# Two attention layers on one core: other credit thresholds for side steps in cross attention, and a longer hold on the keys' staging

## The chip, the cores and the metric

The kernel runs on 1 core of one Trainium2 chip. The metric is the device time of one execution in microseconds (us). A round below is one step of the kernel's main loop, not a measurement. Three timed runs of the kernel before gave 2921.99 (median), 2918.47 and 2926.42 us.

## The reference

Two layers, each with self attention, cross attention and a gated feed-forward part, on x of 4 x 512 x 320 with a context of 4 x 1601 x 192. There are 20 heads of 16 columns.

```python
h1 = _ln(x, n1_g, n1_b)
x = _attn(h1, h1, q1, k1, v1, o1_w, o1_b, heads) + x
h2 = _ln(x, n2_g, n2_b)
x = _attn(h2, context, q2, k2, v2, o2_w, o2_b, heads) + x
h3 = _ln(x, n3_g, n3_b)
a, g = jnp.split(h3 @ ff_w1 + ff_b1, 2, axis=-1)
x = a * gelu(g) @ ff_w2 + ff_b2 + x
```

`_attn` projects queries, keys and values, takes the softmax of the scaled products per head, and projects the result. In cross attention keys and values come from the context, so there are 1601 of them for each of the 4 batch entries.

## The kernel before, in words

**Units.** The work is a list of units (lines 364 to 371). An attention unit, called a visit here, is one batch entry b and one group g of four heads; there are 5 groups, so 20 visits make a layer's self attention and 20 its cross attention. Each head of a group has 32 rows of its own in the arrays, so that four heads run side by side.

**Rounds.** `main` (line 1311) goes through a visit's keys in chunks of 128: 4 rounds in self attention, 13 in cross attention. One round holds

- the scores of the chunk for four heads (`st`, line 1324: two products of keys and queries, in a high and a low part, and one that subtracts the row's maximum), each followed by an exponential on ScalarE into a `pr` tile (line 1334);
- beside them products for the maxima of the next visits (`sps`, lines 1076 and 1101), each reduced on VectorE (lines 1087 and 1111). `giver` (line 1623) hands these out;
- the product of the exponentials of the chunk before with the values (`av`, line 1350), which ScalarE copies out as `vo` (line 1369) and GpSimd adds to `o` (line 1370);
- then the side steps, by `steps(None, ...)` (line 1399).

`clock["round"]` counts half rounds: in cross attention two for each pass of the loop.

**Side steps.** What a visit needs of projections is queued in chains, first in, first out (line 396). The heavy ones run on TensorE and are evacuated by ScalarE or VectorE:

- `keys_of_context` (line 964): a visit's keys in four parts (`kps`, line 972). ScalarE copies each part into the staging `room["halves"]`; after the fourth, GpSimd splits it into a high and a low part (lines 827 and 828), and two DMAs (line 876) carry the halves to the visit's `kT`, once that is free;
- `queries` (line 938, `qps`, line 947), in the same chain behind the visit's keys;
- `values` (line 1025, `vps`, line 1035) of a batch entry, 13 chunks in two parts of 8 and 12 heads. The visits g = 0 and g = 2 read freshly made values, and line 1346 runs whatever is still missing ahead of the `av` that reads it;
- `project` (line 1243, `ops`, line 1250), the output projection, 8 steps for each batch entry.

Each entry has a cost in us of the planner, written into the code, a due date in half rounds, and a test that says whether it can go. Light entries (norms, transposes, DMAs) cost 0.01 or nothing.

**Credit.** `tick` (line 483) adds `pace()` to the credit at each half round, kept between -2 and 4. `pace()` (line 465) is the largest, over all due dates, of the summed cost of the entries due until then divided by the half rounds left. `steps` (line 487) takes the entry that is due first, and runs it if the credit reaches a threshold; running one takes its cost off the credit. In attention rounds the threshold is 0.5 of the entry's cost for the first heavy step of a round, 0.75 for the second, 1.5 for the third, and a credit of 3.0 for any more:

```python
share = (2.2, 1.1) if beside else (9.0, 9.0) if beside is False else (0.5, 0.75, 1.5)
least = cost * share[done] if done < len(share) else 3.0
if clock["credit"] < (3.0 if beside is False else least):
    break
```

**The keys' staging.** There is one. `pending["k"]` counts the moves of keys that are waiting to be issued; the first part of the next visit's keys can go when there are none (`keys_free`, line 890), that is from the moment at which both DMAs have been issued. `carry` (line 808) issues the moves, at the end of `steps`.

Of the kernel before, what the change touches and what calls it, by code (L numbers as in the profile page):

```python
# [78 lines left out]
def kernel(ctx: ExitStack, tc: tile.TileContext, x, context, ws, out):  # L79
# [59 lines left out]
    room = {"turn": 0, "first": 0}  # L139
# [68 lines left out]
    def now(fs):  # L208
        for f in fs:
            f()  # L210
# [183 lines left out]


    chains = {n: deque() for n in ("divide", "project", "norm", "scale", "context", "early", "proj", "values")}
    clock = {"round": 0, "credit": 0.0, "lights": 0, "tiles": None, "ff": False}
    ALIKE = ("project", "early", "proj", "values")
    LIGHT = 0.01
    stage = [0] * B  # L400
# [50 lines left out]
    def pick():  # L451
        heads = [
            (q[0][1] + late_by(n), n)
            for n, q in chains.items()
            if q and q[0][2]() and q[0][3]() and (q[0][0][0] != LIGHT or clock["lights"])
        ]
        return min(heads)[1] if heads else None

    def run(chain):
        costs, _, ready, _, f = chains[chain].popleft()  # L460
        assert ready(), chain
        f()
        clock["credit"] -= sum(costs)
# [19 lines left out]
    def tick():  # L483
        clock["round"] += 1
        clock["credit"] = max(-2.0, min(4.0, clock["credit"] + pace()))

    def steps(beside, lights=1):


        tick()  # L490
        clock["lights"] = lights
        clock["tiles"] = True if beside is None else None
        done = 0
        while True:
            name = pick()
            if name is None:
                break
            cost = sum(chains[name][0][0])
            if cost >= 0.1:
                share = (2.2, 1.1) if beside else (9.0, 9.0) if beside is False else (0.5, 0.75, 1.5)  # L500
                least = cost * share[done] if done < len(share) else 3.0
                if clock["credit"] < (3.0 if beside is False else least):
                    break
                done += 1
                if clock["tiles"] is not None:
                    clock["tiles"] = name in ALIKE
            run(name)
            if cost == LIGHT:
                clock["lights"] -= 1
        clock["tiles"] = None  # L510
        carry()
# [200 lines left out]
    def until_normed(test):  # L712
        while not test():
            if chains["scale"] and chains["scale"][0][2]():
                run("scale")
            elif bands:
                bands.popleft()[1]()
            else:
                run("norm")
# [72 lines left out]
    def lead(u):  # L792

        if u.i == 0:
            return 0
        return units[u.i - (AHEAD - 1 if u.early else 2 if u.m == 0 else 1)].start
# [8 lines left out]
    pending = {"q": 0, "k": 0}  # L805
    movers = []

    def carry():

        room = 4  # L810
        for _, what, u in sorted(movers):
            todo = u.moves[what]
            while todo and todo[0][1]() and clock["round"] >= u.moving[what] + todo[0][2] and room > 0:
                room -= 2
                todo.popleft()[0]()
            if not todo:
                movers.remove((u.i, what, u))
        while errands and room > 0 and clock["round"] >= errands[0][0] and errands[0][1]():
            errands.popleft()[2]()
        few = 6 if clock["ff"] else min(room + 1, 3)  # L820
        while bands and few > 0 and clock["round"] >= bands[0][0]:
            bands.popleft()[1]()
            few -= 1
# [6 lines left out]
    def add_proj(u):  # L830
# [35 lines left out]
        def move(of, pairs, may, gap=0):  # L866

            def f():
                pending[of] -= 1
                u.moving[of] = clock["round"]  # L870
                for to, src in pairs():
                    queue = nc.sync
                    if start["on"]:
                        queue = (nc.sync, nc.scalar)[room["first"] % 2]
                        room["first"] += 1
                    queue.dma_start(out=to.bitcast(F32), in_=src)
                u.open -= 1
                if not u.open:
                    u.when = -9 if start["on"] else clock["round"]

            pending[of] += 1
            u.moves[of].append((f, may, gap))
            u.moving[of] = clock["round"]
            if (u.i, of, u) not in movers:
                movers.append((u.i, of, u))
# [2 lines left out]
            return len(users) < 2 or not users[-2].moves["q"] and (start["on"] or clock["round"] >= users[-2].moving["q"] + 4)  # L888

        def keys_free():  # L890
            return not pending["k"]

        def move_queries(halves, cols, may, gap):
            n = halves.shape[0]
# [384 lines left out]
    def flush():  # L1279
        for f in late:  # L1280
            f()
        late.clear()
# [28 lines left out]
    def main(u, give, nxt):  # L1311
# [62 lines left out]
        for c in range(u.nch):  # L1374
# [21 lines left out]
            if last and c == u.nch - 1:  # L1396
                for _ in range(4):
                    begin(units[u.i + 1])
            steps(None, 1 if extra or c == u.nch - 1 else 2)
            for i, e in enumerate(extra[1:]):  # L1400
                if i and next_cost() is not None:
# [14 lines left out]
    def add_norms(i):  # L1416

        while norms and norms[0].i <= i + ((1 if norms[0].b else 3) if norms[0].kind == "ff" else AHEAD + 1 if norms[0].early else 8):
            u = norms.popleft()
            if u.kind == "ff":  # L1420
                add_norm(u.l, u.b, 2, lambda t, u=u: setattr(u, "hT", t), lambda u=u: u in ff_read, u.start - (4 if u.b else 40))
            else:

                def done(u=u):
                    return u.made["q"] == G and (u.cross or u.made["k"] == G and u.vmade[1] == u.nch)

                due = lead(u) - ((10 if u.early else 12) if u.cross else 28)
                add_norm(u.l, u.b, int(u.cross), lambda t, u=u: u.own.update(h=t), done, due)
# [30 lines left out]
    def ff_main(u, give, nxt):  # L1459
        done = 0  # L1460

        def beside(room, n):

            nonlocal done
            if room:
                for extra in give(done, True)[1]:
                    round_of(extra)
            done += n
            if done == u.steps - 1 and nxt is not None and nxt.kind != "ff":
                max_reduce(nxt)  # L1470
                max_end(nxt)
            steps(True)
            for _ in range(n - 1):
                steps(False)
# [86 lines left out]
    def before(u):  # L1561

        if u.kind == "cross" and u.g == 1 and u.b + 1 < B or u.kind == "self" and u.m == EARLY - 3:
            b = u.b + 1 if u.cross else 0
            if u.l == 0:
                load_context(b, 0)
                load_context(b, 1)
                if u.cross:
                    add_turned(b, u.start + 46, 6)
        if u.kind == "self" and u.m == 0 and u.l:  # L1570
            take_rooms(u.l)
        if u.kind == "cross" and u.m == B * G - 1:
            take_weights()
            loads.extend(load_first(u.l, (0, 1, 3)) + load_ff(u.l)[2])
        if u.kind == "cross" and u.m == B * G - 3:
            take_rests()
            small, rests, _ = load_ff(u.l)
            loads.extend(small + rests)
        if u.kind == "cross" and u.m == B * G - 2:
            loads.extend(load_first(u.l, (4, 2)))  # L1580
        if u.kind == "self" and u.m == EARLY - 1 and u.l == 0:
            add_turned(0, units[u.i + 1].start + 22, 2)
        if u.kind == "self" and u.m == EARLY:

            add_context(0, lambda s: units[u.i - u.m + B * G].own.update(kv=s["cT"]), u.start + 36, yes)
# [142 lines left out]
    for i, u in enumerate(units):  # L1728
        nxt = units[i + 1] if i + 1 < len(units) else None
        before(u)  # L1730
        if u.kind == "ff":

            flush()
            now(loads)
            loads.clear()
            until_normed(lambda: u.hT is not None)
        clock["ff"] = u.kind == "ff"
        add_norms(i)
        for k in (3, SOON, AHEAD):
            v = units[i + k] if i + k < len(units) else None  # L1740
            if v is not None and v.kind != "ff" and k == (SOON if not v.cross else AHEAD if v.early else 3):
                add_proj(v)
                if v.g == 0:
                    add_values(v)
        (ff_main if u.kind == "ff" else main)(u, giver(u), nxt)
# [27 lines left out]
```

## Time and profile before

| | |
|---|---|
| median of 3 timed runs | 2921.99 us (2918.47 to 2926.42) |
| the profiled execution | 2916.39 us, span 2914.6 us |
| mean granted TensorE clock | 0.995 |
| instructions | 83287 |

The span runs from the first instruction to the last. PE is TensorE, PEld its weight loader, which runs beside it; DVE is VectorE, ACT ScalarE, POOL GpSimd, SP the queue that issues the DMAs. A matmul that waits in the pipeline is counted as busy. The lines of a group name the line of the kernel, the engine, the operation, what is written from what is read, and the number of them; then the busy time, the mean of one in ns, and the idle time of the engine before them with what ended it. A line of the timeline gives the start, the time it took, the engine and the instruction, and in brackets the idle time before it with what ended it. A line of the waits gives who waited for whom, the sum in us, the number, and the longest.

By the timeline the self attention of layer 0 takes about the first 370 us of the span. The windows used below, 375 to 1137 us and in layer 1 1915 to 2575 us, hold the cross attention rounds in which side steps still go; behind them the last visits of each layer run without any.

### The profile page before, as it was taken

To read this page: it belongs to the slowest core of one execution; us is meant where nothing else is said; L and a number is where in the kernel's file an instruction comes from. 1 tells how busy PE (TensorE), PEld (TensorE's weight loads), DVE (VectorE), ACT (ScalarE), POOL (GpSimd) and SP (SyncE) were. 2 spreads that over 40 slices of the span, in tenths; PEclk is the share of its full clock that TensorE was granted. 3 is DMA by queue.
4 is the path that set the end of the run, shared out by engine and by line. 5 is a ranking of instruction groups with operands and counts; after the bars stand their busy time and mean duration, and the time that the engine had idled before them with its cause. 6 is when DMAs were issued, how large, how long until landed. Compare 5 with 4: busy or idle time off the path is not lost.

```text
span 2914.6 us, 83287 instructions
## 1 busy us (share of the span) xinstructions
PE 2860.1 (98%) x35018; PEld 1545.0 (53%) x35018; DVE 1975.7 (68%) x3752; ACT 1950.2 (67%) x4033; POOL 1299.4 (45%) x1409
## 2 busy tenths in 40 slices
PE   8999999999999999999999999999999999999999
PEld 4445555555555555355554555555555555544554
DVE  7777888788788878323257678787778878862221
ACT  3777678888888888500138776788888888893000
POOL 3656345555645545211125653455455464551100
PEclk8999999999999999999999999999999999999999
DMA  4444223232132222200113432222221122122000
GB/s 106 114 121 102 72 71 97 58 89 60 48 96 59 55 54 63 85 17 11 36 45 88 109 99 67 61 64 57 54 66 47 50 73 60 45 65 67 23 21 13
DMA packets 163495, 188.59 MB, mean 65 GB/s; under 512 B 61989, under 2 KB 109105, under 8 KB 163121
## 3 DMA queue, kind: packets, MB, share of 16 engines
q1 hardware_dynamic: 162616, 181.69, 24.4%
q8 instruction: 275, 4.51, 0.6%
q10 hardware_dynamic: 472, 1.58, 0.2%
q14 instruction: 100, 0.81, 0.1%
q0 software_dynamic: 32, 0.00, 0.0%
HBM read 55.76 MB, written 29.36 MB: 29 GB/s over the span
## 4 chain that ended last, share of the span: by engine, by line
PE 88%; DVE 4%; POOL 4%; DMA 2%; issue 1%; ACT 1%; SPq 0%; POOLq 0%; ACTq 0%; DVEq 0%
PE av L1350 22%; PE st L1324 20%; PE fps L1435 10%; PE sps L1076 9%; PE yps L1542 6%; PE vps L1035 5%; PE kps L972 4%; PE ops L1250 3%; PE qkps L908 3%; PE fps L1495 3%; DVE nmax L1087 2%; PE qps L947 2%; PE sps L1101 1%; POOL o L1370 1%; DVE pm L1087 1%
## 5 line engine op out<-in xcount | busy, mean ns | idle before, releaser
L1334 ACT ACTIVATE pr<-st 128x512 f32<-128x512 f32 (+1 forms) x2720 | 1405.0, 603 | 321.4 <-PE st L1324 292.0
L1087 DVE TENSOR_REDUCE pm<-sps 128x1 f32<-128x512 f32 (+1 forms) x1920 | 1148.3, 660 | 244.6 <-PE sps L1076 239.0
L1370 POOL TENSOR_TENSOR o<-o,vo 128x512 f32<-128x512 f32 x576 | 739.9, 1285 | 930.3 <-ACT vo L1369 909.7
L1076 PE MATMUL sps<-kT,q 32*128 32x450 f32 (+1 forms) x4800 | 870.6, 422 | 8.1 <-DMA q<-halves 4.4
L1324 PE MATMUL st<-q,kT 32*128 32x512 f32 (+1 forms) x5120 | 788.9, 419 | 0.8 <-ACT o L1364 0.4
L1350 PE MATMUL av<-pr,vals 128*32 128x512 f32 (+1 forms) x5440 | 734.2, 606 | 27.3 <-ACT pr L1334 5.4
L1324 PEld LDWEIGHTS st<-q,kT 32*128 32x128 f32 (+1 forms) x5120 | 447.0, 180 | 293.0 <-issue 112.7
L1324 PE MATMUL st<-nrows,ones 32*128 32x512 f32 (+1 forms) x2720 | 560.6, 398 | 4.5 <-DMA nrows<-turned 4.4
L1087 DVE TENSOR_REDUCE nmax<-sps 128x1 f32<-128x512 f32 x640 | 397.2, 682 | 118.0 <-PE sps L1076 114.2
L1076 PEld LDWEIGHTS sps<-kT,q 32*128 32x128 f32 x4800 | 434.0, 184 | 67.1 <-ACT pr L1334 11.7
L1369 ACT COPY vo<-av 128x512 f32<-128x512 f32 x576 | 351.7, 611 | 14.7 <-PE av L1350 8.7
L1506 ACT ACTIVATE gl<-fps,b 128x512 f32<-128x512 f32 x80 | 54.8, 687 | 408.8 <-PE fps L1495 299.1
L1435 PE MATMUL fps<-hT,w 128*128 128x512 f32 x640 | 283.1, 597 | 0.0
L1350 PEld LDWEIGHTS av<-pr,vals 128*32 128x32 f32 (+1 forms) x5440 | 111.0, 108 | 300.3 <-DVE pm L1087 185.2
L1324 PEld LDWEIGHTS st<-nrows,ones 32*128 32x128 f32 (+1 forms) x2720 | 262.3, 180 | 14.5 <-DMA nrows<-turned 6.1
L1507 DVE SCALAR_TENSOR_TENSOR hid<-fps,b,gl 128x512 f32<-128x512 f32 x80 | 59.7, 748 | 248.1 <-ACT gl L1506 246.0
L1435 PEld LDWEIGHTS fps<-hT,w 128*128 128x128 f32 x640 | 119.2, 190 | 155.1 <-issue 152.2
L1542 PE MATMUL yps<-w,hid 128*128 128x320 f32 x640 | 175.7, 434 | 0.0
L1542 PEld LDWEIGHTS yps<-w,hid 128*128 128x128 f32 x640 | 120.5, 190 | 56.3 <-ACT gl L1506 5.3
L1250 PEld LDWEIGHTS ops<-wo,aT 112*32 112x32 f32 (+1 forms) x3072 | 98.2, 110 | 59.2 <-issue 28.5
L1250 PE MATMUL ops<-wo,aT 112*32 112x160 f32 (+1 forms) x3072 | 123.8, 299 | 3.7 <-POOL aT L1232 2.7
L1111 DVE TENSOR_REDUCE pm<-sps 128x4 f32<-128x508 f32 x160 | 98.9, 680 | 37.5 <-PE sps L1101 34.8
(89 smaller groups left out, 2453.7 us busy)
## 6 DMA issues: line engine op xcount, KB each, us to landing
kT<-stages SPq DMA_DIRECT2D x80, 400.5 KB
oway<-o SPq DMA_DIRECT2D x80, 256.0 KB
q<-halves SPq DMA_DIRECT2D x80, 256.0 KB
q<-halves SPq DMA_DIRECT2D x27, 512.0 KB
kT<-halves SPq DMA_DIRECT2D x40, 256.0 KB
aT<-oway SPq DMA_DIRECT2D x32, 224.0 KB
rT<-rway SPq DMA_DIRECT2D x32, 224.0 KB
hT<-hturned SPq DMA_DIRECT2D x96, 64.0 KB
```

Of the source, the lines that this page charges most:

```text
L972: nc.tensor.matmul(ps[(i * GT + f) * SLOT : (i * GT + f + 1) * SLOT, :w], lhsT=wk2[:, k, u.g * GD + f * SLOT : u.g * GD + (f + 1) * SLOT], ...
L1035: nc.tensor.matmul(ps[f : f + m, :w], lhsT=u.kvT[:n, k, at + f : at + f + m], rhs=wv[:n, k, h0 * DH : h1 * DH], start=(k == 0), stop=(k == ...
L1076: nc.tensor.matmul(own[0][:, :w], lhsT=u.queries(slice(j * SLOT, (j + 1) * SLOT), e, t), rhs=u.kT[j * SLOT : (j + 1) * SLOT, u.k0 + at : u ...
L1087: nc.vector.tensor_reduce(to, own[0][:, :w], AX.X, ALU.max)
L1250: nc.tensor.matmul(ps[f : f + m, : D // 2], lhsT=aT[:n, k, f * NQ + t * SLOT : f * NQ + t * SLOT + m], rhs=wo[:n, k, cols], start=(k == 0) ...
L1324: nc.tensor.matmul(own[0][:r, :], lhsT=ones[rows, :r] if e == 2 else u.keys(rows, c), rhs=u.rows[rows, :] if e == 2 else u.queries(rows, e ...
L1334: nc.scalar.activation(p[:r], own[0][:r], AF.Exp)
L1350: nc.tensor.matmul(ps[j * SLOT : (j + 1) * SLOT, :], lhsT=columns_of[:r, head : head + SLOT], rhs=pr.pop((c, j))[:r, :], start=True, stop= ...
L1369: nc.scalar.copy(vo, ps)
L1370: nc.gpsimd.tensor_tensor(u.o, u.o, vo, ALU.add)
L1435: nc.tensor.matmul(ps, lhsT=w1[:, k, i * FF + c * P : i * FF + (c + 1) * P], rhs=natural(u.hT[:, k]), start=start, stop=stop,)
L1542: nc.tensor.matmul(ps[:, :D], lhsT=hid[c][:, t * P : (t + 1) * P], rhs=w2[:, c, :], start=(c == 0), stop=(c == NHC - 1),)
```

## The change

In cross attention (`clock["cross"]`, set for each unit) the first heavy step of a round goes when the credit is at least -0.5, whatever its cost; a second when the credit left is at least 1.5 times its cost; a third and any further one at a credit of 3.0. The other stages keep their thresholds. And the first part of a visit's keys also waits until four half rounds have gone by since the last move of keys was issued (`room["sent"]`).

```diff
-    clock = {"round": 0, "credit": 0.0, "lights": 0, "tiles": None, "ff": False}
+    clock = {"round": 0, "credit": 0.0, "lights": 0, "tiles": None, "ff": False, "cross": False}
...
                 least = cost * share[done] if done < len(share) else 3.0
+                if beside is None and clock["cross"]:
+                    least = (-0.5, 1.5 * cost, 3.0)[min(done, 2)]
                 if clock["credit"] < (3.0 if beside is False else least):
                     break
...
             def f():
                 pending[of] -= 1
+                if of == "k":
+                    room["sent"] = clock["round"]
                 u.moving[of] = clock["round"]
...
         def keys_free():
-            return not pending["k"]
+            return not pending["k"] and clock["round"] >= room.get("sent", -9) + 4
...
         clock["ff"] = u.kind == "ff"
+        clock["cross"] = u.cross
         add_norms(i)
```

## The prediction

> **What bounds the kernel now.** I read the page first: the busy times, then the chain that ended last.
>
> ```profile
> span 2914.6 us, 83287 instructions
> PE 2860.1 (98%) x35018; PEld 1545.0 (53%) x35018; DVE 1975.7 (68%) x3752; ACT 1950.2 (67%) x4033; POOL 1299.4 (45%) x1409
> PE 88%; DVE 4%; POOL 4%; DMA 2%; issue 1%; ACT 1%; SPq 0%; POOLq 0%; ACTq 0%; DVEq 0%
> ```
>
> TensorE (PE) is busy for 98% of the span and holds 88% of the chain. A queued matmul that waits inside the pipeline still counts as busy, so the next question is how much of this is work. The change acts in cross attention alone, so I took the windows view of the two stretches in which its visits run with side steps.
>
> ```profile
> 375.00:1137.00 762.00, 750.34 (x10924) 418.98 (x10920) 621.32 (x1154) 639.65 (x1354) 408.08 (x388) 1.00 0.27 68
> 1915.00:2575.00 660.00, 654.66 (x9468) 363.85 (x9464) 530.87 (x973) 566.14 (x1199) 364.81 (x353) 1.00 0.23 57
> ```
>
> The columns are PE, PEld, DVE, ACT, POOL. The stretches are 1422 us, half of the span; VectorE (DVE) is busy for 82% and 80% of them, ScalarE (ACT) for 84% and 86%. Three engines are close to full, so an uneven round makes one wait for another. The timeline shows it. Each round begins with the `st` score matmuls, goes on to the four-head `av` product, and then come the side steps (keys `kps`, values `vps`, queries `qps`, output projection `ops`).
>
> ```profile
> 511.03 0.18 PEld L1324 LDWEIGHTS st<-q,kT 32*128 32x128 f32 x2 [0.32 <-issue]
> 513.38 0.86 PE L972 MATMUL kps<-ctxT,w 96*32 96x200 f32 x16
> 514.17 0.18 PEld L1324 LDWEIGHTS st<-q,kT 32*128 32x128 f32 x2 [0.32 <-issue]
> ...
> 624.93 0.18 PEld L1324 LDWEIGHTS st<-q,kT 32*128 32x128 f32 x2 [0.32 <-issue]
> 627.38 0.18 PEld L1324 LDWEIGHTS st<-q,kT 32*128 32x128 f32 x2 [0.84 <-ACT pr L1334]
> 627.85 0.62 ACT L1369 COPY vo<-av 128x512 f32<-128x512 f32 x1
> 628.38 2.06 ACT L1334 ACTIVATE pr<-st 128x512 f32<-128x512 f32 x4
> 630.06 0.86 PE L972 MATMUL kps<-ctxT,w 96*32 96x200 f32 x16
> 630.85 0.13 PEld L1324 LDWEIGHTS st<-q,kT 32*65 32x65 f32 x2 [0.32 <-issue]
> ```
>
> The first three rows are a round with one keys step behind another such round: from `st` to `st`, 511.03 to 514.17, is 3.14 us. From 624.93 to 627.38 no step goes, and the round lasts 2.45 us. The next one, 627.38 to 630.85, again with one keys step, lasts 3.47 us. So an empty round gives back 3.47 - 3.14 = **0.33 us** in the round after it: ACT runs `vo` and four exponentials without a gap, and PE has come too soon for their banks. The work is the same wherever a step stands; 0.33 us is the price of an empty round. The mark of one is the idle time of 0.84 us in the weight loader, against 0.20 to 0.32 us behind a step.
>
> **How many empty rounds, and how many needn't be.** The waits view, weight loader only, in the two stretches and in four windows of the first (540 to 640, 640 to 750, 750 to 840 and 955 to 1030 us):
>
> ```profile
> PEld st L1324 <- ACT pr L1334: 37.3, 48, 0.8
> PEld st L1324 <- ACT pr L1334: 35.1, 44, 0.8
> PEld st L1324 <- ACT pr L1334: 10.3, 13, 0.8
> PEld st L1324 <- ACT pr L1334: 1.7, 2, 0.8
> PEld st L1324 <- ACT pr L1334: 10.1, 12, 0.8
> PEld st L1324 <- ACT pr L1334: 10.3, 13, 0.8
> ```
>
> Each of these waits is either 0.84 us or about 0.3 us. 48 waits that sum to 37.3 us are then (37.3 - 48 x 0.3) / 0.54 = 42 empty rounds; the second stretch has (35.1 - 44 x 0.3) / 0.54 = 41. Rounds and steps come from the groups of instructions in the same stretches (eight `av` matmuls to a round; every step ends in one evacuation):
>
> ```profile
> L1350 PE MATMUL av<-pr,vals 128*32 128x512 f32 (+1 forms) x1864 | 248.2, 605 | 9.8 <-DVE pm L1087 3.3 <-ACT pr L1334 2.3 <-ACT vo L1369 0.3
> L1017 ACT COPY vals<-vps 128x192 f32<-128x192 f32 (+2 forms) x98 | 31.4, 325 | 3.1 <-PE vps L1035 2.3
> L1017 ACT COPY stages<-kps 128x200 f32<-128x200 f32 x71 | 25.4, 358 | 3.9 <-PE kps L972 2.9 <-DMA kT<-stages 0.5
> L1257 DVE TENSOR_TENSOR x<-ops,x 128x160 f32<-128x160 f32 x35 | 11.3, 323 | 9.6 <-PE ops L1250 9.6
> L956 ACT ACTIVATE halves<-qps 128x256 f32<-128x256 f32 x18 | 6.9, 385 | 8.4 <-PE qps L947 8.4
> ...
> L1350 PE MATMUL av<-pr,vals 128*32 128x512 f32 (+1 forms) x1656 | 220.5, 605 | 5.3 <-DVE pm L1087 1.0 <-ACT pr L1334 0.9
> L1017 ACT COPY vals<-vps 128x192 f32<-128x192 f32 (+2 forms) x88 | 28.6, 330 | 2.0 <-PE vps L1035 1.0
> L1017 ACT COPY stages<-kps 128x200 f32<-128x200 f32 (+1 forms) x61 | 21.4, 352 | 3.3 <-PE kps L972 2.7
> L1257 DVE TENSOR_TENSOR x<-ops,x 128x160 f32<-128x160 f32 x23 | 7.3, 318 | 5.0 <-PE ops L1250 5.0
> L956 ACT ACTIVATE halves<-qps 128x256 f32<-128x256 f32 x16 | 6.2, 385 | 7.2 <-PE qps L947 7.2
> ```
>
> First stretch: 1864 / 8 = 233 rounds and 98 + 71 + 35 + 18 = 222 steps. With one step to a round 233 - 222 = 11 would be empty; 42 are, so 31 steps stand as a second or third. Second stretch: 207 rounds, 188 steps, 19 must be empty, 41 are: 22. **53 empty rounds** have a doubled step opposite them.
>
> **The new thresholds.** Credit is in no view, but the code gives the rule. Costs (of chain entries): values 0.48 or 0.69, keys 0.72, output projection 0.95, queries 1.43. Now the first step of a round goes at 0.5 of its cost, a second when 0.75 of its cost is left after the first, that is from 1.75 costs; exactly one goes between. For keys this band is 0.36 to 1.25, 0.9 wide. After the change it runs from -0.5 to 2.5 costs: -0.5 to 1.79 for keys, 2.3 wide; for values of 0.48 it grows from 0.6 to 1.7. A swing of the rate is absorbed by the difference, 1.1 to 1.4 credit, some 2 steps at 0.5 to 0.7 each.
>
> The four windows show the swings: by the same arithmetic 12, 2, 12 and 12 empty rounds. A batch of five visits has one lull and one burst. Each layer has three such lulls and begins with the overload that self attention leaves: four swings, eight in both layers, 2 steps moved by each: 16. Outside the lulls stand 42 - 3 x 12 = 6 empty rounds of the first stretch, and I take as many for the second. Each has its double near it, and the wider band takes nearly all: 12. That is 28 of 53, and 28 x 0.33 = **9.2 us**. Ends: none of them moves (0), all move (53 x 0.33 = 17.5 us).
>
> **The keys' gate.** One transfer `kT<-stages` issued at 946.78 us held the next keys copy on ACT:
>
> ```profile
> 946.78 1.22 SPq L876 DMA_DIRECT2D kT<-stages  x2
> ...
> 954.07 0.33 ACT L1017 COPY stages<-kps 128x201 f32<-128x201 f32 x1 [0.52 <-DMA kT<-stages]
> ```
>
> So the halves are read until 7.3 us after the issue; four half rounds are two rounds, 6.3 us at 3.14 us each. This wait is the group's only DMA wait (0.5 us in its row above), so the gate takes away 0.5 us now, and covers the earlier start that -0.5 would bring. What it holds back: the keys are the head of a first-in-first-out chain with the visit's queries behind them, both later by two rounds at most. A visit's keys take four steps of 13 rounds; I cost this at nothing. If that cover is gone the queries come late, and the maxima of a coming visit go in extra rounds. No instruction and no DMA is added; SP's order shifts only with the steps.
>
> **A side term.** Moved steps move POOL's split of the keys, and DVE's root of a norm can fall into it:
>
> ```profile
> 682.05 1.91 POOL L828 TENSOR_TENSOR stages<-stages 128x801 f32<-128x801 f32 x1
> 682.56 1.43 DVE L521 TENSOR_SCALAR root<-mv 128x4 f32<-128x4 f32 x1
> 686.00 1.07 PE L1350 MATMUL av<-pr,vals 128*32 128x512 f32 x8 [2.02 <-DVE pm L1087]
> ...
> L521 DVE TENSOR_SCALAR root<-mv x24: 156/170/1430, 6.0 to 2810.9; 128x4 f32<-128x4 f32 x24
> ```
>
> A 128x4 operation whose median is 170 ns took 1430 ns, ending as the split ended, and PE stood for 2.0 us. I take 0 for the change in such meetings; its ends are one fewer (-2 us) and two more (+4 us). The Trainium skill ("SBUF — State Buffer", Who interferes with whom) says that VectorE's tensor_scalar can need a port pair that GpSimd holds as an exclusive lock, and that the later one blocks fully. By that rule a meeting depends on the instant alone, and the sum would be as likely to lose as to win here; the row agrees, with 1430 against 170 ns.
>
> **Sum.** -9.2 - 0.5 = -9.7 us on a profiled span of 2914.6 us, so 2904.9. That execution took 2916.39 us, 1.8 us more than its span, and lies 5.6 us below the median 2921.99. On the median: **2912.3 us**.
>
> **Rivals.**
> *The bursts stay.* pace() divides the work left by the time to its due date, so what is held back raises the rate, and what goes early lowers it; the lull keeps its empty rounds, and only those beside a double in a burst go: 12 x 0.33 = 4 us, 2918. For it: 12 empty rounds in a row of visits look like a lack of work, not of smoothness. Against it: in the alternation at 624.93 to 630.85 keys parts of one visit are next in line all the time and are held by credit only. That the change does nothing, steps being short because none is ready, belongs here too: 2922.
> *Forced values, slower.* Held-back second steps let values miss their due date, and line 1346 then runs them directly in front of the `av` that reads them. Place: the visits g = 0 and g = 2, 16 in all. Price, from a usual round:
>
> ```profile
> 604.78 2.06 ACT L1334 ACTIVATE pr<-st 128x512 f32<-128x512 f32 x4 [0.51 <-PE st L1324]
> 605.18 1.06 PE L1350 MATMUL av<-pr,vals 128*32 128x512 f32 x8
> ```
>
> The copy (325 ns in its group's row) would queue behind the exponentials, to 606.84 + 0.33 = 607.17; the `av`, at 605.18 and at most the 0.69 us of a keys step (3.14 - 2.45) later, could start at 605.87. That is 1.3 us for each forced chunk. Eight eat the gain; from 15 the kernel is slower by more than 0.3%. One in each visit: 16 x 1.3 - 9.7 = +11.1, 2933. Against it: the due date is a round ahead of the use, and pace() rises as it comes near.
>
> **How the numbers follow.** A measurement of this kernel tells about 0.3% (8.8 us) from no change: below 2913.2 is faster, above 2930.8 slower. Chances: forecast 0.63 (its own range 2904 to 2917, by 17.5 and 5 us of gain), bursts stay 0.2, forced values or late queries 0.17. The forecast lies close to the limit: of the stretch from 5 to 17.5 us of gain 70% lies beyond 8.8 us, and 0.63 x 0.7 is 0.44, put at 0.45 for faster. The rest of it and the second case make 0.38 the same; the last case is the 0.17 of slower. The range goes from 2901 (all 53, and a lower draw: the runs spread by 3.5 us below the median) to 2927 (no change, 4.4 us above the median as the highest run).
>
> **What would show it.** Right: in the same stretches the weight loader's waits on `pr` fall from 48 and 44 to about 30 each, with values groups of x32 and x48 rare, and rounds of 3.14 us with a keys step unchanged. The first keys copy waits for no `kT` transfer. Wrong: as many 0.84 us gaps as before (bursts stay); ACT `vals` directly ahead of a waiting `av` (forced values); PE waits on DVE in `av` above 4 us in a stretch (side term); or a keys round after an empty one at 3.14 us, by which the price itself falls.

## The result, and the profile after

Five runs of the changed kernel gave 2907.47 us (median; 2904.82 to 2910.41), against 2921.99 before. The ratio is 0.9949, with a 95% interval of 0.9938 to 0.996: 14.5 us less by the medians. The forecast was 2912.3 us and 9.7 us less. The profiled execution took 2907.47 us, its span is 2905.7 us.

The page of the profile after:

```profile
span 2905.7 us, 83278 instructions
PE 2847.9 (98%) x35018; PEld 1540.6 (53%) x35018; DVE 1975.7 (68%) x3752; ACT 1949.3 (67%) x4033; POOL 1301.6 (45%) x1409
```

Each engine runs as many instructions as before, and DVE, ACT and POOL are busy for as long within 2.2 us. PE's busy time, which holds the waits in its pipeline, falls by 12.2 us. The bound is the same; only the order has changed.

**Where the time went.** The kernel has 680 rounds in both versions, so the first `av` of the same round can be compared. Self attention of a layer has 20 x 4 rounds, cross attention 20 x 13. These are the rows of the timeline in which cross attention 0, self attention 1 and cross attention 1 begin, and that of the last round. First the kernel before, then after:

```profile
381.18 0.64 PE L1350 MATMUL av<-pr,vals 128*32 128x512 f32 x4
1505.82 1.08 PE L1350 MATMUL av<-pr,vals 128*32 128x512 f32 x4
1827.69 0.64 PE L1350 MATMUL av<-pr,vals 128*32 128x512 f32 x4
2643.15 0.64 PE L1350 MATMUL av<-pr,vals 65*32 65x512 f32 x4
```

```profile
385.40 0.64 PE L1354 MATMUL av<-pr,vals 128*32 128x512 f32 x4
1500.71 1.08 PE L1354 MATMUL av<-pr,vals 128*32 128x512 f32 x4
1820.16 0.64 PE L1354 MATMUL av<-pr,vals 128*32 128x512 f32 x4
2634.23 0.64 PE L1354 MATMUL av<-pr,vals 65*32 65x512 f32 x4
```

After minus before is +4.22, -5.11, -7.53 and -8.92 us at these four places. So the part ahead of cross attention 0, which the change doesn't touch, was 4.2 us slower in this execution; from there to self attention 1 the change gained 9.3 us, in self attention 1 2.4 us, and in cross attention 1 only 1.4 us. That is 13.1 us in all, near the 14.5 of the medians, while the two spans differ by 8.9. e1 below, whose instructions stand in the same order, gained 9.0, 3.1 and 1.4 us in these parts: two executions of one order differ by up to 0.7 us in a part. Why the first part differs between executions, and what the medians hold beside these 13 us, is told at the end.

**The empty rounds.** The weight loader's waits on `pr` after the change, in the two stretches, 375 to 1137 and 1915 to 2575 us, and in the third row in a lull (540 to 640, 750 to 840 and 955 to 1030 us have the same row each):

```profile
PEld st L1328 <- ACT pr L1338: 31.3, 44, 0.8
PEld st L1328 <- ACT pr L1338: 29.7, 38, 0.8
PEld st L1328 <- ACT pr L1338: 8.6, 11, 0.8
```

By the prediction's formula, sum less 0.3 us a wait, over 0.54, the stretches have 33.5 and 33.9 empty rounds, where they had 42.4 and 40.6: 16 fewer. A lull has (8.6 - 11 x 0.3) / 0.54 = 10, where it had 12.

The groups of the first stretch, after:

```profile
L1354 PE MATMUL av<-pr,vals 128*32 128x512 f32 (+1 forms) x1888 | 251.6, 605 | 8.6 <-ACT pr L1338 3.1 <-DVE pm L1091 1.3
L1021 ACT COPY vals<-vps 128x192 f32<-128x192 f32 (+2 forms) x98 | 31.9, 329 | 6.0 <-PE vps L1039 5.8
L1021 ACT COPY stages<-kps 128x201 f32<-128x201 f32 (+1 forms) x72 | 25.9, 360 | 1.8 <-PE kps L976 1.3
L1261 DVE TENSOR_TENSOR x<-ops,x 128x160 f32<-128x160 f32 x37 | 11.9, 321 | 8.4 <-PE ops L1254 8.4
L960 ACT ACTIVATE halves<-qps 128x256 f32<-128x256 f32 x18 | 6.9, 385 | 7.0 <-PE qps L951 7.0
```

Read as in the prediction: 1888 / 8 = 236 rounds, 225 steps, 11 rounds that must be empty and 33.5 that are. Some 22 steps stand as a second one, where there were 31. The copies of the keys no longer wait for a transfer.

How a stretch looks in which an alternation of empty and doubled rounds stood before (624.93 to 630.85 us there); the weight loader's rows at the start of four rounds in a row, after:

```profile
627.89 0.18 PEld L1328 LDWEIGHTS st<-q,kT 32*128 32x128 f32 x2 [0.32 <-issue]
631.02 0.13 PEld L1328 LDWEIGHTS st<-q,kT 32*65 32x65 f32 x2 [0.32 <-issue]
633.43 0.18 PEld L1328 LDWEIGHTS st<-q,kT 32*128 32x128 f32 x2 [0.84 <-ACT pr L1338]
636.87 0.18 PEld L1328 LDWEIGHTS st<-q,kT 32*128 32x128 f32 x2 [0.32 <-DVE pm L1091]
```

The round from 627.89 has one keys step and lasts 3.13 us. The one from 631.02 is empty, 2.41 us, and the keys round behind it lasts 3.44 us. The price of an empty round is unchanged; there are fewer of them.

### The profile page after: what moved, and what is told of

Read it like the earlier page. It is cut to its first block, busy times and chain, and to the rows that moved or that the text cites. A ratio compares the mean times of both kernels' runs of the same rounds, so it can differ in the third digit from the quotient of the medians.

```text
span 2905.7 us, 83278 instructions
## 1 busy us (share of the span) xinstructions
PE 2847.9 (98%) x35018; PEld 1540.6 (53%) x35018; DVE 1975.7 (68%) x3752; ACT 1949.3 (67%) x4033; POOL 1301.6 (45%) x1409
## 4 chain that ended last, share of the span: by engine, by line
PE 87%; DVE 6%; POOL 3%; DMA 1%; issue 1%; ACT 1%; SPq 1%; ACTq 0%; POOLq 0%; DVEq 0%
PE av L1354 22%; PE st L1328 20%; PE fps L1439 10%; PE sps L1080 8%; PE yps L1546 6%; PE vps L1039 5%; PE ops L1254 4%; PE kps L976 3%; PE qkps L912 3%; DVE nmax L1091 3%; PE fps L1499 3%; PE qps L951 2%; DVE pm L1091 2%; PE sps L1105 1%; POOL o L1374 1%
## 5 line engine op out<-in xcount | busy, mean ns | idle before, releaser
L1080 PE MATMUL sps<-kT,q 32*128 32x450 f32 (+1 forms) x4800 | 860.6, 419 | 11.0 <-DMA q<-halves 5.0
```

The lines of the kernel that those rows point to most:

```text
L1080: nc.tensor.matmul(own[0][:, :w], lhsT=u.queries(slice(j * SLOT, (j + 1) * SLOT), e, t), rhs=u.kT[j * SLOT : (j + 1) * SLOT, u.k0 + at : u ...
```

## Experiments

The theory on record was a sum of counts: each empty round costs 0.33 us. With 16 fewer it gives 5.3 us, where 13 to 15 were measured. The rival is that single long stalls in rounds that the edit moves make up the rest, and that these may go or come. Where a round is said to have lost time, it is its length from `st` to `st` less that of usual rounds with the same steps. Ratios are to the kernel before.

**The parts of the change.** e1 is the changed kernel without the keys' gate:

```diff
-            return not pending["k"] and clock["round"] >= room.get("sent", -9) + 4
+            return not pending["k"]
```

> The new thresholds without the keys' gate. In the program's own order the gate then changes no instruction: PE, DVE, ACT, POOL and SP stand as in the changed kernel. Theory A (the time goes with the number of cross attention rounds that have no side step, 0.33 us each; 92 before, 72 now by the order of the program): the same as the changed kernel, ratio 0.995 to before, with its profile within 3 us of 2905.7. Rival C (the gate carries the gain): 0.998 or more. How far two profiles of one program lie apart is read here too.

Measured: 2906.13 us, ratio 0.9948 [0.9935, 0.996]. Its instructions stand in the same order as in the changed kernel, on every engine: with the new thresholds no keys step came up while the gate held. e6 is the kernel before with the gate alone:

```diff
-            return not pending["k"]
+            return not pending["k"] and clock["round"] >= room.get("sent", -9) + 4
```

> The kernel before with the four half rounds between keys' loading and their first copy, its thresholds kept. The prediction put the removed wait of ScalarE at 0.5 us: ratio 0.9998. Theory that this part has no effect on the time: within 0.15% of 1.0. Against it, a theory that half of the gain is due to staging: ratio 0.9975.

Measured: 2919.59 us, 0.9995 [0.9986, 1.0004]: no effect that shows. So the gain is the thresholds'. e2 changes the first alone, e3 the second and third alone, both with the gate:

```diff
-                    least = (-0.5, 1.5 * cost, 3.0)[min(done, 2)]
+                    least = (-0.5, 0.75 * cost, 1.5 * cost if done == 2 else 3.0)[min(done, 2)]
```

> First step at -0.5, second and further steps at the old 0.75, 1.5 and 3.0; gate kept. The order has 77 rounds without a step (92 before, 72 after). Theory A: 15 x 0.33 = 5 us of the 6.6 us that empty rounds give, so some 2909 to 2917, ratio 0.9955 to 0.9985. Theory B (the gain is in a few long stalls that the shift happened to miss, VectorE's root under GpSimd's split of the keys and the late visit of the first batch): no relation to the count; anything from 0.995 to 1.0, told by the PE waits on DVE.

```diff
-                    least = (-0.5, 1.5 * cost, 3.0)[min(done, 2)]
+                    least = (0.5 * cost, 1.5 * cost, 3.0)[min(done, 2)]
```

> First step at the old 0.5 of its cost, second at 1.5 of its cost, further ones at 3.0; gate kept. The order has 83 rounds without a step. Theory A: 9 x 0.33 = 3 us less than before, 2916 to 2921, ratio 0.998 to 1.0. Theory B: anything from 0.995 to 1.0, with the long stalls deciding.

Measured: 2920.06 us, 0.9993 [0.9984, 1.0003], and 2914.72 us, 0.9975 [0.9966, 0.9983]. The weight loader's waits in the two stretches, e2 first and then e3:

```profile
PEld st L1328 <- ACT pr L1338: 35.2, 52, 0.8
PEld st L1328 <- ACT pr L1338: 31.1, 45, 0.8
```

```profile
PEld st L1328 <- ACT pr L1338: 36.0, 47, 0.8
PEld st L1328 <- ACT pr L1338: 31.3, 42, 0.8
```

That is 14 and 8 fewer empty rounds than before, 4.7 and 2.6 us by count. e2 gained 2.0 us and e3 7.3 us, and together they don't make the 15.2 us of e1. Theory A missed on both sides, with e2 above its 2917 and e3 below its 2916. The first threshold takes away more empty rounds and gains less: the count doesn't order these kernels.

**The count driven to both ends.** e4 lets the first step go always; e7 turns the thresholds the other way:

```diff
-                    least = (-0.5, 1.5 * cost, 3.0)[min(done, 2)]
+                    least = (-9.0, 1.5 * cost, 3.0)[min(done, 2)]
```

> The first step of a round goes at any credit (threshold -9), second and third as in the change. The order has 40 rounds without a step, 32 fewer than the changed kernel, and 13 rounds with two. Theory A: 32 x 0.33 = 10.6 us below the changed kernel, 2895 to 2899, ratio 0.991 to 0.992. Theory B: within 5 us of the changed kernel on either side, 2902 to 2913. A third outcome, steps so early that keys or queries wait for their staging: ACT waits on kT or q transfers above 2 us and a time above 2910.

```diff
-                    least = (-0.5, 1.5 * cost, 3.0)[min(done, 2)]
+                    least = (cost, 0.0, 0.0)[min(done, 2)]
```

> The changed kernel with the thresholds of cross attention turned the other way (first step only at a full cost of credit, any second or third step at 0.0): the program's order then has 138 and 139 empty rounds in the stretches where the kernel before has 47 and 45. If an empty round costs 0.33 us whatever stands around it: 185 x 0.33 = 61 us above the kernel before, ratio 1.021. If the price is an artefact of the few rounds that it was read from, or falls where every second round is empty: below half of that, under 30 us, ratio under 1.01. If doubled steps cost a bound of their own beside the empty ones: over 80 us.

Measured: e4 2920.41 us, 0.9998 [0.9989, 1.0007]; e7 2967.7 us, 1.0159 [1.0145, 1.0173]. The waits in the two stretches, e4 and then e7:

```profile
PEld st L1328 <- ACT pr L1338: 16.5, 29, 0.8
PEld st L1328 <- ACT pr L1338: 14.9, 24, 0.8
```

```profile
PEld st L1328 <- ACT pr L1338: 100.9, 123, 0.8
PEld st L1328 <- ACT pr L1338: 93.7, 114, 0.8
```

e7 has 228.7 empty rounds that show the gap, 145.7 more than before (fewer than the order of the program has, since some stand in rows of two or more). 0.0159 x 2922 = 46.5 us over 145.7 is **0.32 us each**. This is an average, and it holds what single stalls e7 has: by the waits of PE, the `av` products stand 9.6 us behind reductions in the two stretches, where it was 4.3 before, and without these 5.3 us it is 0.28. By the 185 of the program's order it is 0.25, and the 61 us that were expected from these were not reached. So the price holds, as 0.25 to 0.32, far beyond the few rounds that it was read from. e4 has 54.3 fewer, 17.9 us at 0.33, and shows no gain. Neither theory had that; nor do waits for the staging explain it, with 1.1 us of ACT on the keys' transfer. Part of where they went, in two rows of e4:

```profile
637.82 0.51 DVE L587 STREAM_TRANSPOSE hturned<-hn 128x320 f32<-128x320 f32 x1 [2.57 <-POOL hn L579]
638.89 1.61 PE L1354 MATMUL av<-pr,vals 128*32 128x512 f32 x8 [2.30 <-DVE pm L1091]
```

A transpose of the next norm stands at the head of DVE's queue and waits for POOL; the reduction `pm` behind it comes late, and PE stands for 2.30 us. This happens in the round from 635.16 us, and again with the same 2.57 us in the round from 2079.79; they last 6.56 and 6.84 us, and lose about 3.5 and 3.8. Light steps such as this transpose follow the heavy ones in the order, so whoever moves the heavy ones moves them too. Further rounds of e4 lose time: 2.3 us in the one from 858.52, where a transpose of the context waits 2.50 us for a transfer, and about 1 us in each of eight.

**A milder step.** e8 has -1.4 as the first threshold, e11 adds a condition that keeps a transpose of the context away from the save that frees its buffer:

```diff
-                    least = (-0.5, 1.5 * cost, 3.0)[min(done, 2)]
+                    least = (-1.4, 1.5 * cost, 3.0)[min(done, 2)]
```

> The changed kernel with the first threshold at -1.4 instead of -0.5; the second stays at one and a half costs. By the program's order 34 and 34 empty rounds instead of 37 and 35, 21 and 20 doubled instead of 24 and 21. If the count decides: 4 x 0.33 = 1.3 us below the changed kernel, ratio to the kernel before 0.9945. If the long stalls of single places decide, as with the first step allowed always: anywhere from 4 us below to 10 us above, ratio 0.993 to 0.998, with the places to be seen in the trace.

```diff
             dma(out=saved[b][:, :, c0 * 32 : (c0 + n) * 32], in_=s[i][:, :, : n * 32])
+            room["saved", i % 2] = clock["round"]
...
-            add("context", LIGHT, lambda i=i: turn(i), at, yes, lambda i=i: clock["round"] >= ctx_in[b, i][1] + 4)
+            add("context", LIGHT, lambda i=i: turn(i), at, yes, lambda i=i: clock["round"] >= ctx_in[b, i][1] + 4 and clock["round"] >= room.get(("saved", i % 2), -9) + 8)
```

> The kernel with the first threshold at -1.4, with one more condition: a transpose of the context goes eight half rounds or more after the save of the one that used its buffer. By the program's order the empty rounds are the same (34 and 34). In the trace with -1.4 such a transpose stood on VectorE for 3.7 us behind a save's transfer, and the rounds at 858.22 and 864.56 lost 3.09 and 1.71 us. Theory that single long waits ate the gain of the fewer empty rounds: 4.8 us less than with -1.4 alone, ratio to the kernel before 0.9970. Rival that the wait moves to another place: no change, 0.9986.

Measured: e8 2918.11 us, 0.9986 [0.9977, 0.9995]; e11 2920.25 us, 1.0 [0.999, 1.0009]. e8's waits in the two stretches, and the rows at its worst round:

```profile
PEld st L1328 <- ACT pr L1338: 29.4, 43, 0.8
PEld st L1328 <- ACT pr L1338: 28.0, 39, 0.8
```

```profile
862.40 0.64 DVE L759 STREAM_TRANSPOSE stages<-stages 128x192 f32<-128x192 f32 x2 [3.72 <-DMA ctxT<-stages]
863.60 0.61 PE L1254 MATMUL ops<-wo,aT 112*32 112x160 f32 x12 [2.66 <-DVE pm L1091]
```

There are 22 fewer empty rounds than before, 7.3 us by count, and 4.1 us were gained: 11 us less than the changed kernel gains with 16 fewer. DVE's transpose waits 3.72 us for a transfer, and PE 2.66 us for the reduction behind it. In e11 that stall is gone, and this row of it shows another in its place:

```profile
890.91 0.69 PE L1329 MATMUL st<-nrows,ones 32*128 32x512 f32 x2 [1.65 <-DMA nrows<-turned]
```

The maxima of the coming visit had not landed; that round, from 888.53, lost 3.9 us. My expectation of 4.8 us gained by the spacing failed, and its rival, that the wait moves, holds.

**One stall put back.** In the kernel before, the queries of the first visit of batch entry 1 went at half round 252 and their maxima took an extra round; the changed kernel issues them at 250. e5 is the changed kernel with these queries held:

```diff
-            add(chain, (0.477,) * 3, queries, due - (4 if u.g == 0 and not u.early else 2), staging_free)
+            add(chain, (0.477,) * 3, queries, due - (4 if u.g == 0 and not u.early else 2), lambda: staging_free() and (u.i != 25 or clock["round"] >= 252))
```

> The changed kernel, with the queries of one visit (the first of the second batch in the first cross attention) held until half round 252, where the kernel before issues them; the changed kernel issues them at 250. By the program's order this brings back one extra round of the maxima ahead of that visit (3 in the layer instead of 2) and 2 empty rounds (39 and 35 instead of 37 and 35). If only the count of empty rounds matters: 2 x 0.33 = 0.7 us more than the changed kernel, ratio to the kernel before 0.995. If the stalls of 1.07, 0.69, 0.84 and 1.06 us around that visit in the trace of the kernel before come from its late queries: 3.7 + 0.7 = about 4 us more, ratio 0.9965, and stalls of that size stand again around 547 and 585 us.

Measured: 2912.39 us, 0.9969 [0.9957, 0.9981], 4.9 us above the changed kernel by the medians. Starts of the rounds concerned, of the kernel before and then of e5:

```profile
583.47 0.18 PEld L1324 LDWEIGHTS st<-q,kT 32*128 32x128 f32 x2 [0.32 <-DVE pm L1087]
587.61 0.18 PEld L1324 LDWEIGHTS st<-q,kT 32*128 32x128 f32 x2 [0.84 <-DVE pm L1087]
591.54 0.13 PEld L1324 LDWEIGHTS st<-q,kT 32*65 32x65 f32 x2 [0.20 <-issue]
```

```profile
587.49 0.18 PEld L1328 LDWEIGHTS st<-q,kT 32*128 32x128 f32 x2 [0.84 <-ACT pr L1338]
591.65 0.18 PEld L1328 LDWEIGHTS st<-q,kT 32*128 32x128 f32 x2 [0.84 <-ACT pr L1338]
595.61 0.13 PEld L1328 LDWEIGHTS st<-q,kT 32*65 32x65 f32 x2 [0.20 <-issue]
```

The two long rounds of before, 4.14 and 3.93 us, stand in e5 again, 4.16 and 3.96. Cross attention 0 and self attention 1 begin in e5 at these rows:

```profile
386.06 0.64 PE L1354 MATMUL av<-pr,vals 128*32 128x512 f32 x4
1505.64 0.64 PE L1354 MATMUL av<-pr,vals 128*32 128x512 f32 x4
```

Between them lie 1119.58 us; it is 1115.31 in the changed kernel and 1124.64 in the one before. Of the 9.3 us gained there, e5 gives 4.3 back. But e5 puts back more than that visit's maxima: some 40 rounds have other steps than in the changed kernel, and another stall of the kernel before comes back with them. A transpose of the context waits on DVE for a transfer, in the kernel before and then in e5:

```profile
653.17 0.64 DVE L757 STREAM_TRANSPOSE stages<-stages 128x192 f32<-128x192 f32 x2 [2.00 <-DMA ctxT<-stages]
654.21 0.64 DVE L759 STREAM_TRANSPOSE stages<-stages 128x192 f32<-128x192 f32 x2 [2.44 <-DMA ctxT<-stages]
```

The round around it loses 1.3 us before (from 650.70) and 1.8 us in e5 (from 651.32); in the changed kernel this transpose doesn't wait. So about 4 us of the gain came with the queries of one visit going two half rounds earlier, the wait of the context included. How much of it is the late maxima alone was not separated.

**The roots.** In e9 and e10 the three DVE operations that begin a root are written in another form, in the changed kernel and in the kernel before:

```diff
-        nc.vector.tensor_scalar(a, var, EPS, None, ALU.add)
-        nc.vector.tensor_scalar(
-            z.bitcast(I32), a.bitcast(I32), 1, None, ALU.logical_shift_right
-        )
-        nc.vector.tensor_scalar(y.bitcast(I32), z.bitcast(I32), -1, 0x5F3759DF, ALU.mult, ALU.add)
+        nc.vector.tensor_tensor(a, var, rooted[:, 0], ALU.add)
+        nc.vector.tensor_tensor(z.bitcast(I32), a.bitcast(I32), rooted[:, 1].bitcast(I32), ALU.logical_shift_right)
+        nc.vector.tensor_tensor(y.bitcast(I32), rooted[:, 2].bitcast(I32), z.bitcast(I32), ALU.subtract)
```

> The changed kernel with the three VectorE operations that begin a root (128x4 each) written as tensor_tensor with constants in tiles, in place of tensor_scalar; nothing else in its order of work. In the trace of the changed kernel such operations took 700 to 1083 ns where the median is 170, while a GpSimd operation ran, at 478.65, 684.5, 2114.09 and 2321.96 us of the stalled rounds, which lost 0.75, 0.38, 1.30 and 1.29 us. Theory that the form of the operation is what has to wait for GpSimd: the four go, 3.7 us less than the changed kernel, ratio to the kernel before 0.9937, and no root operation above 300 ns in the cross attentions. Rival that any small VectorE operation waits there, or that another operation waits in its place: no change, ratio 0.9949.

> The same edit in the kernel before. There the stalled rounds with a long root operation are at 682.55 (2.02 us), 891.96 (1.29) and 1106.45 (1.18). Theory that the form has to wait: 4.5 us less than the kernel before, ratio 0.9985. If so, about 0.8 us (4.5 - 3.7) of what the change gained came from roots that met GpSimd less. Rival: no change, ratio 1.0.

> The kernel with -1.4, the spaced transposes and the roots by tensor_tensor. With -1.4 alone the rounds with a long root operation lost 0.83 (479.65), 1.03 (685.52), 0.92 (898.70) and 1.93 us (2123.10), 4.7 together. If both fixes hold: 4.8 + 4.7 = 9.5 us less than with -1.4 alone, about 2908.6 us, ratio 0.9954, and still no better than the changed kernel, because rounds at 644.31 and 2085.69 (0.95 and 0.98) and smaller ones remain. If with the long waits gone the count of empty rounds decides again: 4 x 0.33 = 1.3 us below the changed kernel with the same roots, ratio 0.993.

Measured: e9 2906.65 us, 0.9955 [0.9942, 0.9967]; e10 2920.92 us, 0.9998 [0.9989, 1.0008]; e12, which is e11 with the same roots, 2917.53 us, 0.9989 [0.998, 0.9998]. No gain from the roots shows in any: e12 lies 2.7 us below e11, but its runs had a mean clock of 0.9947 against 0.9933, which makes 2.3 us by the line at the end. One place in the changed kernel's timeline, and the same in e9's:

```profile
2113.92 1.29 POOL L1374 TENSOR_TENSOR o<-o,vo 128x512 f32<-128x512 f32 x1 [2.17 <-ACT vo L1373]
2114.16 1.08 DVE L523 TENSOR_SCALAR root<-mv 128x4 f32<-128x4 f32 x1
2115.15 0.87 POOL L829 CAST stages<-stages 128x801 fp32r<-128x801 f32 x1
2115.28 0.76 DVE L524 TENSOR_SCALAR root<-root 128x4 int32<-128x4 int32 x1
2116.82 1.06 PE L1354 MATMUL av<-pr,vals 128*32 128x512 f32 x8 [1.30 <-DVE pm L1091]
```

```profile
2114.53 1.28 POOL L1376 TENSOR_TENSOR o<-o,vo 128x512 f32<-128x512 f32 x1 [2.17 <-ACT vo L1375]
2114.76 1.07 DVE L527 TENSOR_TENSOR root<-mv,rooted 128x4 f32<-128x4 f32 x1
2115.86 0.76 DVE L528 TENSOR_TENSOR root<-root,rooted 128x4 int32<-128x4 int32 x1
2117.41 1.06 PE L1356 MATMUL av<-pr,vals 128*32 128x512 f32 x8 [1.28 <-DVE pm L1093]
```

The first two DVE operations of the root each end with the POOL operation beside them, in either form. The theory that the form has to wait fell. No kernel of these beats the changed one: e1 and e9 are level with it.

## Why the prediction was right, and where it was wrong

- *The bound and the price of an empty round: right.* 0.33 us was forecast; the rows after give 3.44 - 3.13 = 0.31, and e7 0.32 over 146 rounds, or 0.25 to 0.28 as told there.
- *The count: wrong.* The step "the wider band takes nearly all: 12" failed. The forecast was 28 fewer, 16 from swings and 12 outside the lulls. The three lulls of the first stretch lost two each, just as "2 steps moved by each" swing said; outside them 6.4 became 33.5 - 3 x 9.8 = 4.1, not none. The overload behind self attention, counted as a fourth swing, shows no such loss. Measured: 16 fewer, 16 x 0.33 = 5.3 us in place of 9.2. The sign that was named for it, waits from 48 and 44 down to about 30 each, didn't come: they are 44 and 38.
- *The gate: no gain of its own.* The forecast gave it 0.5 us. The wait of 0.52 us is gone after, but also by the thresholds alone (e1 has the same order), and e6 shows no effect.
- *The side term: its size about right.* Rounds with a long root lost 2.02 + 1.29 + 1.18 = 4.5 us before and 0.75 + 0.38 + 1.30 + 1.29 = 3.7 after, some at other places, as the rule had it that the instant decides. The net 0.8 us lies close to the 0 of the sum.
- *What the sum didn't have.* The forecast treated a visit with late queries as a danger of the change only; the kernel before had one such visit, and the change mended it: 4.3 us by e5, in which the wait of the context's transpose is counted. And a round shortly ahead of cross attention 1, from 1783.67 us before, lasts 8.02 us there and 5.61 after, with the round ahead of it 0.3 longer: 2.1 us. The kernel before waited 0.76 us in it for the maxima's transfer. The transfers around it are issued in the same order, and why they landed earlier is open.
- *The sum.* 5.3 + 4.3 + 0.8 + 2.1 = 12.5 us, beside the 13.1 that the aligned rows give. The forecast's 9.7 us came out of a main term that was too large and other terms that were missing, so that its number came as near as it did was in part luck. That layer 0 gained 9.3 us and cross attention 1 only 1.4 us, with 9 and 7 fewer empty rounds, shows how much the single stalls weigh. But part by part the terms close less well than in the total: in layer 0 the empty rounds, e5 and the roots make 2.9 + 4.3 + 3.4 = 10.6 us beside the 9.3, and in cross attention 1 7 x 0.33 = 2.3 us stand against two new rounds of 1.3 us at the roots, which leaves -0.3 beside the 1.4. A single term is uncertain by as much.
- *The rivals.* "The bursts stay" was half right: ten of twelve empty rounds in a lull did stay, and its 4 us lies nearer to the 5.3 than the 9.2 does, though in the first stretch most of the rounds that went, 6 of 9, were in lulls and not beside bursts. Forced values played no part. A slower mechanism existed, though another than the one described: light steps that put a long wait at the head of DVE's queue (e4, e8).

Open in part: why the second and third thresholds alone (e3) gained more (7.3 us) than their 8 empty rounds explain (2.6 us), and the first alone (e2) less. The traces show the single stalls of above at work. The two rounds of the late visit, 4.14 and 3.93 us before, last 4.17 and 4.80 us in e2 (from 588.73) and 3.26 and 2.90 at the same place in e3 (from 584.61); the round ahead of cross attention 1, 8.02 us before, lasts 6.31 in e2 and 5.62 in e3. That fits their order; no run puts these stalls back one by one.

## What to carry to other kernels

A cost per event that is read from a few rounds can be sound and still not give the time, when a reordering also moves steps that put waits at the head of an in-order queue. Count the long stalls of before one by one, ask of each whether the new order would still have it, and put them in the sum with the small price times the count. To find them, align two traces by a common event and not by time; and take a threshold found in this way as a fit to one order of work, since -0.5 gained 15 us with the second at 1.5 costs, -1.4 gained 4, and -9 nothing that shows.

## What the runs showed of the hardware

Small DVE operations of 128x4, whose median is 161 to 170 ns, took up to 1430 ns beside a POOL operation, and two in a row can each wait for another one. Two operations of 0.17 us then hold the reduction behind them until PE stands 1.3 us. I had expected tensor_tensor to go free. The Trainium skill ("SBUF — State Buffer", Who interferes with whom) says that a VectorE instruction with two inputs in SBUF contends with a GpSimd instruction that reads SBUF, and e9 agrees, with 1.07 us where 0.16 is usual.

The spread between runs of one kernel follows the granted clock. Over 189 runs of the kernels here the mean clock lies between 0.990 and 0.997, and a straight line through the runs of each kernel, with one slope for all, gives 1.6 us more for each 0.001 less (correlation -0.76). This bears on the gain: e1's five runs had 0.9956 in the mean, the 27 of the kernel before beside them 0.9937. By that line 3 us of the 15.9 between their medians are the clock's, and the 13 that are left are what the aligned rows give. Whether the kernel has a part in its clock isn't known. The clock is lost at the start. The windows view, 0 to 375 us, of the kernel before and of e6, with the granted clock in the third column from the right:

```profile
0.00:375.00 375.00, 352.36 (x4942) 189.71 (x4946) 282.09 (x586) 246.00 (x502) 185.05 (x221) 0.97 0.39 101
```

```profile
0.00:375.00 375.00, 350.61 (x4790) 188.09 (x4790) 274.71 (x569) 239.74 (x488) 183.69 (x220) 0.95 0.39 100
```

At 0.95 the same work is behind by 152 of 4942 matmuls, and the profiled span of e6 is 8.6 us above that of before although its median is below. So a difference of a few us between two profiles must be taken stretch by stretch.
